# Opening PSUM sums by ScalarE copies and splitting B in place, in a hybrid state-space and attention kernel

## The chip, the cores and the metric

The kernel runs on one core of a Trainium2 chip. The metric is the device time of one execution in microseconds (us). The five engines are called by their short names: PE (TensorE, matmuls; its weight loads are PEld), DVE (VectorE), ACT (ScalarE), POOL (GpSimd) and SP (SyncE, which issues all the DMAs). SBUF is the working memory; PSUM is the small memory of 8 banks that matmuls write and add into.

## The reference

The network has four layers over an image batch of shape (4, 64, 64, 96). Layers 0 and 1 are selective state-space blocks, layers 2 and 3 are linear attention with a quantised feed-forward block. Nearly all of the time is in layers 0 and 1. Layer 0, cut to what matters (layer 1 differs in its four orders of the pixels):

```python
xz = x @ in_proj_w.T
xi, z = jnp.split(xz, 2, axis=-1)
xc = silu(conv3x3_depthwise(xi) + conv_b)             # 192 channels, 4096 pixels
xs = four orders of xc                                # rows, columns, and both reversed
dts, Bs, Cs = jnp.split(einsum('bkdl,kcd->bkcl', xs, x_proj_w), [R, R + N], axis=2)
delta = softplus(einsum('bkrl,kdr->bkdl', dts, dt_w) + dt_b)

def step(h, inp):                                     # N = 16 states per channel
    u_t, dt_t, B_t, C_t = inp
    h = exp(dt_t[..., None] * A) * h + (dt_t * u_t)[..., None] * B_t[:, :, None, :]
    return h, einsum('bkdn,bkn->bkd', h, C_t)

out_y = ys + Ds * xs
y = sum of the four orders of out_y, each put back in image order
y = layer_norm(y) * silu(z) @ out_proj_w.T
```

The sum over the four orders k of `Ds * xs` is, in image order, `(sum of Ds over k) * xc`. The sum y of a pixel thus starts from that product and takes in 4 orders of 16 states each.

## The kernel before, in words

**Tiling.** Two images share the 128 partitions, 64 channels each, and the 192 channels make J = 3 chunks j. A phase is one of the two layers with one pair of images, so there are 4 phases. In a phase the loops run over k (4 orders) and t (4 stretches of TB = 1024 pixels); one (phase, k, t) is a block, 64 in all. A block has 48 tiles: two groups g of 8 states, for each the chunks j, and in each of those 8 tiles n. A tile of 128 x 1024 holds two states of one image. That makes 3072 tiles, and a **boundary** after every 8 tiles, 384 sums in all.

**One tile i** passes through these instructions, each on a fixed engine:

- the decay `exp(delta * a)`, ACT, line 692 (`decays`), into the tile f or, for 5 of 16 states (`POOL_N` = 1, 4, 7, 10, 13), into PSUM psB;
- the input `du * B`. For the 11 other states PE spreads the row of B over the partitions into psB (line 685, `row`, a bf16 matmul with selector weights), and DVE multiplies by du (line 699, `product`). For the 5 of `POOL_N`, POOL multiplies with rows that a DMA spread (line 675, `begin`);
- the scan along the 1024 pixels, DVE, line 707, and a copy of its last column for the next block, ACT, line 713;
- the weighting by C, POOL, line 718 (`weigh`), in place in f. There are 6 buffers of f;
- after every second tile, the gather: PE adds the two states of both tiles into the sum tile psY (line 750, 4 fp32 matmuls, 8 instructions in the records).

**The sum tile.** psY takes two PSUM banks, and there is one of it. The other six banks are two psB of two banks each and two psM of one bank each. After 8 tiles `flush` copies psY out on ACT: after the first group into an SBUF tile ysum (line 762); after the second back into image order into ynew (line 766, in one to four pieces by the order) and on to DRAM. Then `resume` reopens psY for the next group with what was summed before, by matmuls with `start=True` (line 741, PE): ysum with the identity for g = 1; for g = 0, the old sum yold, which a DMA brought in (`recall`, line 727), in the order of this k, again with the identity; and for the first k the conv's output, with the diagonal matrix dg of summed Ds.

**Order of the work.** PE, DVE, ACT and POOL execute their instructions in the order in which the program writes them; only SP's order is left to the scheduler. The main loop, at step i, writes: the decay of tile i+2 (`begin`), the flush of i-3 if it ends a group, the gather of i-2 (for odd n), the row of i+2, the scan of i, the POOL_N decay of i+2, the product of i+1, the weighting of i, then the preparation of the next block (`prepare`, a table of places in the block), a piece of the aside work, and last of all `resume` of i-2 if that begins a group. The aside work is the convolution of a later phase and the layer norm, gate and output projection of the one before; it needs psM tiles, and takes none during the places at which `prepare` needs them.

**The split of B.** `prepare` projects xs to B, C and dt rows in a psM tile (line 565), copies them out (`rows`, line 576), and cuts B into three bf16 parts whose sum is B (`cut`, line 582, ACT). Between the cuts `take` makes the remainder: a fresh psM tile, B in fp32 by the identity (line 587), minus the parts so far (line 588). The `steps` (line 592) with `biased` (599) and softplus (605) give delta, `inputs` (608, POOL) gives delta times x.

After the last tile come the attention and feed-forward layers, written by a small planner at build time that uses the same PSUM tiles.

Of the kernel before, what the change touches and what calls it, by code (L numbers as in the profile page):

```python
# [8 lines left out]
F32 = mybir.dt.float32  # L9
# [8 lines left out]
N = 16  # L18
# [16 lines left out]
def kernel(ctx: ExitStack, tc: tile.TileContext, ins, out, layers=(0, 1, 2, 3)):  # L35
# [8 lines left out]
    def st(shape, dtype, tag, bufs, name=None):  # L44
        return sp.tile(shape, dtype, tag=tag, name=name or tag, bufs=bufs)
# [7 lines left out]
    def psM(shape):  # L53
        return ps.tile(shape, F32, tag="psM", name="psM", bufs=2)
# [18 lines left out]
    def small(shape, name, dtype=F32):  # L73
        return st(shape, dtype, name, 2, name)
# [74 lines left out]

    def skips(li):  # L150

        dsum = small([128, J, 1], "dsum")
        nc.vector.reduce_sum(dsum, W[li]["ds"], axis=mybir.AxisListType.X)
        dg = W[li]["dg"] = st([128, J, 128], F32, "dg", 1)
        for j in range(J):
            nc.scalar.activation(dg[:, j, :], ident, AF.Copy, scale=dsum[:, j, :])

    def tail_weights(li):

# [312 lines left out]
    def pieces(li, k, t):  # L472

        if li == 0:
            if k in (0, 2):
                tt = t if k == 0 else NTB - 1 - t
                img = lambda v: v[:, tt * TB : (tt + 1) * TB]
                view = lambda v: v if k == 0 else v[:, ::-1]  # L480
                return img, [(view, lambda o: o)], lambda py, v: [
                    (py[:, s * T : (s + 1) * T], view(v)[:, s * T : (s + 1) * T]) for s in range(2)
                ]
            cols = TB // HW
            tt = t if k == 1 else NTB - 1 - t
            img = lambda v: v.rearrange("p (h w) -> p h w", w=HW)[:, :, tt * cols : (tt + 1) * cols]

            def view(v):
                v = v.rearrange("p h w -> p w h")
                return v if k == 1 else v[:, ::-1, ::-1]  # L490

            return img, [(view, lambda o: o.rearrange("p (w h) -> p w h", h=HW))], lambda py, v: [
                (py[:, s * T : (s + 1) * T], view(v)[:, s * cols // 2 : (s + 1) * cols // 2]) for s in range(2)
            ]
        img = lambda v: v[:, t * TB : (t + 1) * TB]
        if k == 0:
            return img, [(lambda v: v, lambda o: o)], None
        s = 1 << k
        n = TB // (s * HW)

        def by_row(r):
            return (
                lambda v: v.rearrange("p (a i b j) -> p i a b j", i=s, j=s, b=HW // s)[:, r],
                lambda o: o.rearrange("p (a b i j) -> p i a b j", i=s, j=s, b=HW // s)[:, r],
            )

        def by_band(a):
            return (
                lambda v: v.rearrange("p (a i b j) -> p a b i j", i=s, j=s, b=HW // s)[:, a],
                lambda o: o.rearrange("p (a b i j) -> p a b i j", i=s, j=s, b=HW // s)[:, a],  # L510
            )

        def resumed(py, v):
            v = v.rearrange("p (a i b j) -> p a b i j", i=s, j=s, b=HW // s)
            return [(py[:, a * TB // n : (a + 1) * TB // n], v[:, a]) for a in range(n)]

        return img, [by_row(r) for r in range(s)] if s < n else [by_band(a) for a in range(n)], resumed

    def imaged(li, k, v):

# [2 lines left out]
    def prepare(ph, k, t):  # L523
# [2 lines left out]


        li = phases[ph][0]
        img, views, resumed = pieces(li, k, t)
        p = {"views": views, "img": img, "resumed": resumed, "dus": [None] * J, "deltas": [None] * J}  # L530
        xs, deltas = [], []
        halves = [slice(s * T, (s + 1) * T) for s in range(2)]
        raws, pps, rests, pds = [], [], [], []
        taken = {}

        def weights():
            if li not in W:
                W[li] = scan_weights(li)
            if t == 0 and k == 0 and "dg" not in W[li]:
                skips(li)  # L540
            if t == 0:
                xp = st([128, J, 76], F32, "xp", 1)
                nc.sync.dma_start(xp, ins[f"L{li}_xp"][k])
                dtw = st([76, J, 128], F32, "dtw", 1)
                nc.sync.dma_start(dtw[64:76], ins[f"L{li}_dtw"][k])
                order[0] = (xp, dtw)
# [31 lines left out]
            nc.sync.dma_start(p["bc"][:, halves[s]], rests[s][0 : 4 * N])  # L578

        def cut(s, q):  # L580
            of = taken.pop(s) if q else pps[s][0 : 2 * N]
            nc.scalar.copy(p["parts"][32 * q : 32 * q + 32, halves[s]], of)

        def take(s, q):
            of = taken[s] = psM([2 * N, T])
            part = slice(0, 32 * q + 32)
            nc.tensor.matmul(of, ident[0 : 2 * N, 0 : 2 * N], rests[s][0 : 2 * N], start=True, stop=False)
            nc.tensor.matmul(of, minus[part], p["parts"][part, halves[s]], start=False, stop=True)

        def steps(s, j):  # L590
            pds.append(psM([128, T]))
# [128 lines left out]

    def recall(i):
        at, g, j, n = tiles[i]
        ph, k, t = blocks[at]
        sums[at, j] = imaged(phases[ph][0], k, part([128, TB], "yold"))
        nc.sync.dma_start(sums[at, j], made[at]["img"]((yd if k else xcd)[ph][:, j, :]))

    def resume(i):
        at, g, j, n = tiles[i]  # L730
        ph, k, t = blocks[at]
        py = sums[at, g, j] = psY()
        old = sums.pop((at, j))
        of = W[phases[ph][0]]["dg"][:, j, :] if g == 0 and k == 0 else ident
        if g == 0 and k:
            parts = made[at]["resumed"](py, old)
        else:
            parts = [(py[:, s * T : (s + 1) * T], old[:, s * T : (s + 1) * T]) for s in range(2)]
        banks = len(parts) * T // TB
        for m, (o, v) in enumerate(parts):  # L740
            nc.tensor.matmul(o, of, v, start=(m % banks == 0), stop=False)  # L741

    def gather(i):
        at, g, j, n = tiles[i]
        py = sums[at, g, j]
        two = [scanned.pop(e)[1] for e in (i - 1, i)]
        for s in range(2):
            ss = slice(s * T, (s + 1) * T)
            for e in range(2):
                nc.tensor.matmul(  # L750
                    py[64 * e : 64 * e + 64, ss], fold, two[e][:, ss],
                    start=False, stop=(n == g * GN + GN - 1),
                )

    def flush(i):
# [283 lines left out]
    end = len(tiles)  # L1039
    now, rest = [0], (L - TB) // 256  # L1040
    with tc.manual_schedule(engines=MANUAL):
        convs = [conv(0)]
        while done[0][0] < TB // T:
            next(convs[0])
# [24 lines left out]
        for i in range(-9, end + 4):  # L1069
# [5 lines left out]
                begin(i + 2)  # L1075
            if 0 <= i - 3 < end and tiles[i - 3][3] % GN == GN - 1:
                flush(i - 3)
            if 0 <= i - 2 < end and tiles[i - 2][3] % 2:
                gather(i - 2)
            if 0 <= i + 2 < end:  # L1080
# [11 lines left out]
            if 0 <= i < end:  # L1092
# [21 lines left out]
                if aside is not None and not (plan and place in kept) and (holds[0] or holds[1] <= room):  # L1114
                    advance()
                    if holds[2] and (late_by(i, blocks[at][0]) or holds[0] >= room):
                        advance()
            if 0 <= i - 2 < end and tiles[i - 2][3] % GN == 0:
                resume(i - 2)
        now[0] = end + per  # L1120

        def remaining():
# [113 lines left out]
```

## Time and profile before

| what | value |
|---|---|
| median of 3 runs | 11,311.74 us (11,305.0 to 11,312.93) |
| the profiled execution | 11,302.74 us |
| its span, from the first instruction to the last | 11,301.0 us |
| scan stage, first to last weighting | 139 to 10,674 us |
| POOL busy | 10,203.7 us |
| DVE busy | 9,943.6 us |
| PE busy | 9,004.1 us |
| ACT busy | 6,635.3 us |
| granted TensorE clock, mean | 0.856 |

The page gives, per engine, the time in which it executed something; an engine that waits for another is idle. A row of the groups names the line, the engine, the operation and the tiles written and read, then the count, the busy time and the mean of one in ns, and behind the bar the idle time of the engine ahead of those instructions with what ended most of it. The matmul times include the pipeline, so neighbours overlap a little. An fp32 matmul shows as two instructions.

### The profile page before, as it was taken

The page shows a single profiled execution, that of the slowest core. Times are in us where ns is not written, and L with a number is a line of the kernel's source. Part 1 is how long each engine was busy: PE and PEld are TensorE (multiplying, and loading weights), DVE is VectorE, ACT ScalarE, POOL GpSimd, SP SyncE. Part 2 cuts the span into 40 slices and gives each one's busy share as a digit, 9 for nine tenths or more (in the row PEclk, how much of TensorE's full clock was granted, in tenths as well). Part 3 has the DMA queues.
Part 4 walks back from the last instruction along what each step waited for, and adds up shares of the span by engine and source line. Part 5 has one row for each costly group of instructions (what it writes and reads, how often), then busy time and mean ns, then how long its engine had stood idle before and what let it go on. Part 6 is the DMA issues. An engine that isn't in the chain of part 4 may idle for free. (4 is left out here: it accounts for less than half of the span.)

```text
span 11301.0 us, 102140 instructions
## 1 busy us (share of the span) xinstructions
PE 9004.1 (80%) x30112; PEld 2910.9 (26%) x30112; DVE 9943.6 (88%) x6431; ACT 6635.3 (59%) x10733; POOL 10203.7 (90%) x5102
## 2 busy tenths in 40 slices
PE   7878888777777877888777777888778887777776
PEld 2212222111222222222222222222222232222365
DVE  4888999999999899988999999999989899999835
ACT  3656666554556655666555655666555555555676
POOL 3889999999999999989999998999999999999846
PEclk8989898888888888988888888999888888888877
DMA  5669876897678886799656556665566565556410
GB/s 131 154 137 158 141 154 155 152 135 135 151 162 143 140 159 155 152 142 148 149 146 159 156 138 150 159 167 146 143 157 156 140 157 146 138 139 154 123 39 18
DMA packets 1848989, 1605.36 MB, mean 142 GB/s; under 512 B 1412330, under 2 KB 1483692, under 8 KB 1848428
## 3 DMA queue, kind: packets, MB, share of 16 engines
q1 hardware_dynamic: 1848428, 1598.83, 65.1%
q8 instruction: 237, 3.88, 0.2%
q14 instruction: 324, 2.65, 0.1%
HBM read 1009.16 MB, written 186.65 MB: 106 GB/s over the span
## 5 line engine op out<-in xcount | busy, mean ns | idle before, releaser
L718 POOL TENSOR_TENSOR f<-f,crep 128x1024 f32<-128x1024 f32 x3072 | 7165.4, 2356 | 522.9 <-DVE f L707 413.0
L707 DVE TENSOR_TENSOR_SCAN f<-f,state,psB 128x1024 f32<-128x1024 f32 x1584 | 3718.0, 2347 | 210.4 <-ACT f L692 48.0
L750 PE MATMUL psY<-f,fold 128*64 128x512 f32 x12288 | 3771.4, 701 | 161.0 <-POOL f L718 160.3
L692 ACT ACTIVATE f<-delta,L_a 128x1024 f32<-128x1024 f32 x2112 | 2408.6, 1145 | 988.1 <-PE psY L750 897.8
L699 DVE TENSOR_TENSOR psB<-psB,du 128x1024 f32<-128x1024 f32 x2112 | 2558.5, 1211 | 458.9 <-PE psB L685 405.1
L685 PE MATMUL psB<-spB,sel 96*128 96x512 bf16 x4224 | 1406.9, 420 | 1626.0 <-DVE f L707 1595.8
L675 POOL TENSOR_TENSOR f<-du,brep 128x1024 f32<-128x1024 f32 x960 | 2266.9, 2361 | 169.5 <-DMA crep<-bc 39.2
L707 DVE TENSOR_TENSOR_SCAN f<-psB,state,f 128x1024 f32<-128x1024 f32 x720 | 1677.0, 2329 | 123.7 <-ACT psB L692 86.6
L713 ACT COPY state<-f 128x1 f32<-128x1 f32 x2304 | 430.4, 187 | 2048.2 <-DVE f L707 2037.5
L750 PEld LDWEIGHTS psY<-f,fold 128*64 128x64 f32 x12288 | 952.7, 155 | 2524.2 <-issue 1818.0
L692 ACT ACTIVATE psB<-delta,L_a 128x1024 f32<-128x1024 f32 x960 | 1070.7, 1115 | 625.0 <-DVE f L707 576.8
L707 DVE TENSOR_TENSOR_SCAN f<-f,psB 128x1024 f32<-128x1024 f32 x528 | 1207.6, 2287 | 55.1 <-ACT f L692 5.1
L685 PEld LDWEIGHTS <-sel 96*128 96x128 bf16 x4224 | 274.5, 99 | 3320.8 <-DVE f L707 2106.4
L300 PE MATMUL psM<-pad,wf 96*64 96x512 f32 x3456 | 872.7, 622 | 7.1 <-ACT pad L290 4.0
L741 PE MATMUL psY<-ysum,ident 128*128 128x512 f32 x768 | 589.5, 912 | 73.3 <-ACT ynew L766 60.2
L707 DVE TENSOR_TENSOR_SCAN f<-psB,f 128x1024 f32<-128x1024 f32 x240 | 545.7, 2274 | 78.4 <-ACT psB L692 46.5
L608 POOL TENSOR_TENSOR xs<-delta,xs 128x1024 f32<-128x1024 f32 x192 | 453.0, 2359 | 93.6 <-ACT delta L605 93.6
L741 PE MATMUL psY<-yold,ident 128*128 128x512 f32 (+2 forms) x960 | 388.5, 547 | 129.9 <-ACT ysum L762 98.3
L592 PE MATMUL psM<-proj,dtw 12*128 12x512 f32 x768 | 456.5, 688 | 0.0
L565 PE MATMUL psM<-xs,xp 128*76 128x512 f32 x768 | 417.7, 655 | 10.1 <-DMA xp<-in_L_xp 4.1
L766 ACT COPY ynew<-psY 128x1024 f32<-128x1024 f32 (+2 forms) x312 | 242.3, 818 | 188.7 <-PE psY L750 188.7
L300 PEld LDWEIGHTS psM<-pad,wf 96*64 96x64 f32 x3456 | 223.5, 139 | 475.9 <-issue 448.0
(150 smaller groups left out, 6946.9 us busy)
## 6 DMA issues: line engine op xcount, KB each, us to landing
crep<-bc SPq DMA_DIRECT2D x2048, 256.0 KB
delta<-delta SPq DMA_DIRECT2D x768, 256.0 KB
du<-xs SPq DMA_DIRECT2D x768, 256.0 KB
brep<-bc SPq DMA_DIRECT2D x640, 256.0 KB
yd<-ynew SPq DMA_DIRECT2D x192, 512.0 KB
xraw<-xcd SPq DMA_DIRECT2D x144, 512.0 KB
yold<-yd SPq DMA_DIRECT2D x144, 512.0 KB
yu<-yd SPq DMA_DIRECT2D x65, 384.0 KB
```

The costliest lines, as they stand in the source:

```text
L300: nc.tensor.matmul(px[64 * i : 64 * i + 64], w["wf"][:, tap, 64 * j : 64 * j + 64], pads[i][0][:, tap // 3 : tap // 3 + rows, tap % 3 : ta ...
L592: nc.tensor.matmul(pds[-1], order[0][1][64:76, j, :], rests[s][64:76], start=True, stop=True)
L608: nc.gpsimd.tensor_mul(xs[j], deltas[j], xs[j])
L675: nc.gpsimd.tensor_mul(f[:, 1:], made[at]["dus"][j][n % 2], reps[at, 0, n])
L685: nc.tensor.matmul(scanned[i][0][:, ss], sel[:, n, :], made[at]["parts"][:, ss], start=True, stop=True)
L692: nc.scalar.activation(out, made[at]["deltas"][j][n % 2], AF.Exp, scale=W[phases[ph][0]]["a"][:, k, j, n // 2 : n // 2 + 1])
L699: nc.vector.tensor_mul(scanned[i][0], scanned[i][0], made[at]["dus"][j][n % 2])
L707: nc.vector.tensor_tensor_scan(f[:, 1:], a, bu, 0.0 if t == 0 else states[at - 1][:, c : c + 1], ALU.mult, ALU.add)
L713: nc.scalar.copy(states[at][:, c : c + 1], f[:, TB : TB + 1])
L718: nc.gpsimd.tensor_mul(f[:, 0:TB], f[:, 1:], reps[at, 1, n])
L741: nc.tensor.matmul(o, of, v, start=(m % banks == 0), stop=False)
L750: nc.tensor.matmul(py[64 * e : 64 * e + 64, ss], fold, two[e][:, ss], start=False, stop=(n == g * GN + GN - 1),)
```

## The change

- `resume` no longer uses PE. ACT writes the old sum into psY: a plain copy of ysum for g = 1; a copy with the scale dsum, one number per partition, for g = 0 of the first k; and for g = 0 of the other k one to four copies that read yold in this k's order. The gathers then add to what ACT wrote, with `start=False`.
- `resume` is written right after the flush in the step, ahead of the gather, and no longer at its end.
- `unlock` runs once at the start: 8 matmuls of the identity over psY, so that the later matmuls with `start=False` add to what is in the banks.
- The matrices dg (3 activations for each of the two layers) are no longer made; the sums dsum are kept.
- `take` no longer uses a second psM tile nor the identity matmul. It subtracts the one part cut last from the projection itself, in its PSUM tile, and the next cut reads it there.
- In the instruction streams DVE and POOL have the same instructions in the same order; PE loses 960 matmuls of resumes and 256 of takes and gains the 8; ACT gains 504 copies. SP issues the same 5,798 DMAs with some in other places.

```diff
     def skips(li):
-        dsum = small([128, J, 1], "dsum")
+        dsum = W[li]["skip"] = small([128, J, 1], "dsum")
         nc.vector.reduce_sum(dsum, W[li]["ds"], axis=mybir.AxisListType.X)
-        dg = W[li]["dg"] = st([128, J, 128], F32, "dg", 1)
-        for j in range(J):
-            nc.scalar.activation(dg[:, j, :], ident, AF.Copy, scale=dsum[:, j, :])
...
         def cut(s, q):
-            of = taken.pop(s) if q else pps[s][0 : 2 * N]
-            nc.scalar.copy(p["parts"][32 * q : 32 * q + 32, halves[s]], of)
+            nc.scalar.copy(p["parts"][32 * q : 32 * q + 32, halves[s]], pps[s][0 : 2 * N])
 
         def take(s, q):
-            of = taken[s] = psM([2 * N, T])
-            part = slice(0, 32 * q + 32)
-            nc.tensor.matmul(of, ident[0 : 2 * N, 0 : 2 * N], rests[s][0 : 2 * N], start=True, stop=False)
-            nc.tensor.matmul(of, minus[part], p["parts"][part, halves[s]], start=False, stop=True)
+            part = slice(32 * q, 32 * q + 32)
+            nc.tensor.matmul(
+                pps[s][0 : 2 * N], minus[part], p["parts"][part, halves[s]], start=False, stop=True,
+                skip_group_check=True,
+            )
...
+    def unlock():
+        py = psY()
+        for s in range(2):
+            for q in range(T // 128):
+                o = s * T + q * 128
+                nc.tensor.matmul(py[:, o : o + 128], ident, ident, start=(q == 0), stop=True, skip_group_check=True)
...
     def resume(i):
         py = sums[at, g, j] = psY()
         old = sums.pop((at, j))
-        of = W[phases[ph][0]]["dg"][:, j, :] if g == 0 and k == 0 else ident
-        if g == 0 and k:
-            parts = made[at]["resumed"](py, old)
+        if g:
+            nc.scalar.copy(py, old)
+        elif k == 0:
+            nc.scalar.activation(py, old, AF.Copy, scale=W[phases[ph][0]]["skip"][:, j, :])
         else:
-            parts = [(py[:, s * T : (s + 1) * T], old[:, s * T : (s + 1) * T]) for s in range(2)]
-        banks = len(parts) * T // TB
-        for m, (o, v) in enumerate(parts):
-            nc.tensor.matmul(o, of, v, start=(m % banks == 0), stop=False)
+            for src, dst in made[at]["views"]:
+                nc.scalar.copy(dst(py), src(old))
...
+        unlock()
         convs = [conv(0)]
...
                 flush(i - 3)
+            if 0 <= i - 3 < end and tiles[i - 3][3] % GN == GN - 1 and i - 2 < end or i == 2:
+                resume(i - 2)
             if 0 <= i - 2 < end and tiles[i - 2][3] % 2:
                 gather(i - 2)
...
-            if 0 <= i - 2 < end and tiles[i - 2][3] % GN == 0:
-                resume(i - 2)
```

## The prediction

> **What bounds the kernel now.** I read the busy times first, then the same over the scan stage alone (from the first weighting at 139 us to the last at 10,674 us, with the tail and attention after it), then the groups, the waits, and one stretch of the timeline.
>
> ```profile
> PE 9004.1 (80%) x30112; PEld 2910.9 (26%) x30112; DVE 9943.6 (88%) x6431; ACT 6635.3 (59%) x10733; POOL 10203.7 (90%) x5102
> ```
> ```profile
> 139.00:10674.00 10535.00, 8461.81 (x26558) 2505.68 (x26557) 9626.13 (x5543) 6170.27 (x9610) 9843.73 (x4338) 0.86 0.69 149
> ```
>
> The columns of the second are length, then PE, PEld, DVE, ACT, POOL busy, then the granted clock. In the stage POOL is idle 10,535 − 9,844 = 691 us and DVE 909 us. Neither the order nor the work of these two changes, so **691 us is the most that a better feed can give** unless work on them gets shorter. PE at 80% is no bound by its sum; it matters by being late.
>
> ```profile
> L718 POOL TENSOR_TENSOR f<-f,crep 128x1024 f32<-128x1024 f32 x3072 | 7165.4, 2356 | 522.9 <-DVE f L707 413.0
> ...
> L750 PE MATMUL psY<-f,fold 128*64 128x512 f32 x12288 | 3771.4, 701 | 161.0 <-POOL f L718 160.3
> ...
> L699 DVE TENSOR_TENSOR psB<-psB,du 128x1024 f32<-128x1024 f32 x2112 | 2558.5, 1211 | 458.9 <-PE psB L685 405.1
> ...
> L741 PE MATMUL psY<-ysum,ident 128*128 128x512 f32 x768 | 589.5, 912 | 73.3 <-ACT ynew L766 60.2
> ```
>
> The last field is idle time ahead of the group and who ended it. POOL waits for DVE's scan (413 us); DVE waits for PE's row broadcast L685 (405 us). Why is PE late? At a group boundary (every 8 tiles, 384 in all) PE reopens the sum by identity matmuls (L741) after ScalarE has emptied the one psY tile (L762, L766), and in PE's order the next gather L750 and the row L685 stand behind that. One such place on the timeline, PE first, then DVE, then POOL:
>
> ```profile
> 5758.77 3.78 PE L741 MATMUL psY<-ysum,ident 128*128 128x512 f32 x4 [2.46 <-ACT ynew L766]
> 5762.48 3.11 PE L750 MATMUL psY<-f,fold 128*64 128x512 f32 x8
> 5765.52 0.61 PE L685 MATMUL psB<-spB,sel 96*128 96x512 bf16 x2
> ```
> ```profile
> 5761.30 2.35 DVE L707 TENSOR_TENSOR_SCAN f<-psB,state,f 128x1024 f32<-128x1024 f32 x1 [1.10 <-ACT psB L692]
> 5766.17 1.23 DVE L699 TENSOR_TENSOR psB<-psB,du 128x1024 f32<-128x1024 f32 x1 [2.52 <-PE psB L685]
> ```
> ```profile
> 5770.74 2.35 POOL L718 TENSOR_TENSOR f<-f,crep 128x1024 f32<-128x1024 f32 x1 [2.15 <-DVE f L707]
> ```
>
> Columns: start, length, engine, line; in brackets the idle time before and its releaser. The flush L766 had run from 5757.72 to 5758.71. The reopening takes 3.78 us, the gather ends 8 us after the flush began, the product waits 2.52 us for the row behind it, and POOL 2.15 us soon after.
>
> **The change, part by part.**
>
> *The opening moves from PE to ACT.* In the trace's records I paired each of 383 boundaries' flush, reopening and gather. The reopening starts 1.09 us after the flush ended (mean) and lasts 2.82 us. The gather begins with its end every time, on average 4.3 us after the weightings it needs were finished: the reopening is the last input at 382 of 383. Now a ScalarE copy follows the flush at once; the gather waits for that copy instead, and queued behind the gather on PE is, as before, the row L685, for which DVE's product waits. ScalarE into PSUM is seen as L692 psB (1.115 us, Exp), the reverse copy as L762 (1.006 us); permuted flushes L766 as 1.36 us mean (120), 0.58 (512 columns), 0.38 (256 columns). Taken: 240 plain at 1.006; 72 of layer 0 permuted at 1.6 (from L766: (120×1.359 − 48×1.006)/72); layer 1: 96 pieces at 0.58, 96 at 0.379. Sum 241 + 115 + 56 + 36 = **448 us more on ACT** (59% to 63%). With 1.0 or 1.6 us per boundary the gather can begin 2.43 us earlier on average.
>
> Not all of it stays. From the instructions of tile psY:
>
> ```profile
> L750 PE MATMUL psY<-f,fold x12288: 590/592/1117, 145.9 to 10675.4; 128*64 128x512 f32 x199
> ...
> L741 PE MATMUL psY<-ysum,ident x768: 590/1057/1223, 269.8 to 10657.9; 128*128 128x512 f32 x192
> ```
>
> Shortest, median and longest in ns: the ysum reopening mostly runs at half clock, the gather behind it at full. Half of all reopenings (50%) took over 2.9 us. Without them the gather is the first work after PE's wait and takes 3.6 us for 2.08: 0.5×1.5 = 0.7 us lost, 1.72 us left per boundary.
>
> What is felt: I followed every idle gap of POOL in the stage back over its releasers for 16 us. 218 gaps, 271 us, pass through L741, at 135 boundaries. Cutting each boundary at what its gather's end can gain leaves 200 us. Another input is late next (the aside work on PE, ACT's exponentials), so I take 85%: **−170 us**. Ends: 0 (all hidden behind those) and −271.
>
> The trace's clock record shows 487 drops to half in the stage, 2,854 us (27%), in multiples of 3.41 us; PE was busy 42% of the 3.41 us before a drop, 81% at random places. The Trainium skill, "TensorE: Matmul & The Clock Gate", Part 1, says that the clock halves after an idle window of about 3.4 us. The window's length agrees; that it must be idle does not, a thinly used one is enough here. By the page's rule removing reopenings would cost no clock and the term would be 85% of 247, −210; by the rows it is the −170 above, and that speaks against the change.
>
> *ACT's queue.* Behind the new copy wait the state copy L713, the decays L692, cuts L582 and the aside work's copies. I pushed each boundary's following ACT instructions by the copy until idle time took it up, and compared each exponential's end with its scan's start: 83 scans are pushed, 65 us together (in the place above, the 1.10 us wait at 5761.30 becomes about 2.1). Part falls where POOL has work in hand: **+40**, ends 0 and +65. The copy itself waits for nothing new: psY is freed by the same engine, and the loads of yold were issued 12.7 us or more (median 35) before the flush's end, with no wait on them shown.
>
> *take: one matmul for two.* 256 times the fp32 identity matmul L587 goes (512 instructions, 272 us busy, 0.53 us each), and L588 adds onto the projection; it waits for the cut before it, as it did. The chain cut–take–cut stands between a projection and the steps; DVE gaps whose chain (10 us back) holds L588 sum to 69 us, POOL's to 11. Taken: **−25**, ends 0 and −69. The projection's psM tile is held longer, until the third cut, but nothing of the aside work runs in those places.
>
> *At nothing:* the dg tile's 6 activations; unlock's 16 matmul instructions (at L367's 287 ns 4.6 us) lie before 17.03 us, PE's first work, and would cost those 4.6 us if PE were needed then. SP's order: 2,031 of 5,798 issues change place, 99% by 10 or fewer. POOL's waits ended by a DMA sum to 83 us, DVE's to 46; I take 0, ends ±40.
>
> Sum: −170 + 40 − 25 = −155. The profiled execution took 11,302.74 us (span 11,301.0), so 11,148; the median of the runs is 9 us higher, and every case below stands against that median of 11,311.7. **Forecast 11,157 us.**
>
> **The rivals.**
> - *Cold gathers.* With 1,357 us less work (1,085 + 272) PE falls to half clock more often and every gather runs cold: 1.5 us lost at each boundary. The capped sum is then 185 us; with rows late too, half is felt: −93 + 40 − 25 = −78, **11,234**. For it: the 42%; against: in conv blocks PE stays full.
> - *PE's backlog goes.* The aside convolutions and tails queue on PE, and 1,357 us less lets half of the 691 idle go: −346, **10,966**. For it: counted by block, POOL idles some 2 us in blocks without aside work (the ninth to thirteenth, say) and about 10 in those with it. Against: most gaps do not pass through L741.
> - *ACT takes PE's place, slower.* Right behind the flush, where softplus or conv copies keep ACT full, the exponential of a POOL tile comes late by the whole copy, and the scan with it. From 195 us of pushed scans (170 + 25, 43% of the copies) the gain is gone; the trace has 65. At 70%, 314 − 195 = +119: **11,431**. For it: exponential n=4 has under 0.21 us of slack before its scan in a tenth of the tiles; against: its median is 1.9 us.
> - *No change.* The instruction streams do what the diff says, but the product may wait anyway, for the previous scan or the weighting: the −170 shrinks to −20, the −25 to nothing, and of the +40 some 20 remain: 0, **11,312**.
>
> **How the numbers follow.** Forecast 0.44, cold gathers 0.20, backlog 0.13, ACT 0.15, no change 0.08. About 0.2% (23 us) can be told from no change: faster 0.76, same 0.09, slower 0.15. The range goes from 10,970 (all of the 271 and the 69 and no loss: −340) to 11,340 (the same −170, with ACT's pushes at three times 65: +195, so +25); it leaves out most of ACT's case and about half of the backlog's.
>
> **What would show it.** Right: no matmul between flush and gather; gathers beginning 1 to 2 us after the flush's end; L699's wait for L685 falling from 405 us to some 250; POOL's stage idle from 691 to about 540; L750's mean rising above 701 ns. Wrong: L707's wait for ACT L692 growing from 188 us by over 150; or POOL's idle staying at 690 with another releaser.

## The result and the profile after

The changed kernel takes 11,298.22 us in the median (11,281.56 to 11,319.88, 20 runs), the kernel before, on the same chip, 11,302.02 us (11,290.81 to 11,313.71, 20 runs). The ratio is 0.9998, 95% interval 0.9991 to 1.0005: **no change** that can be measured, where 11,157 us was forecast. The profiled execution took 11,291.57 us (span 11,289.8).

First the busy times, then the scan stage alone (columns as before: length, PE, PEld, DVE, ACT, POOL busy, granted clock):

```profile
PE 8418.7 (75%) x27696; PEld 2658.3 (24%) x27696; DVE 9945.0 (88%) x6431; ACT 7094.3 (63%) x11231; POOL 10199.5 (90%) x5102
```
```profile
136.00:10668.00 10532.00, 7883.93 (x24136) 2256.42 (x24137) 9626.61 (x5544) 6630.09 (x10111) 9837.11 (x4338) 0.82 0.68 149
```

ACT's busy time grew by 459 us (448 were worked out). PE's fell by only 585 us, though the matmuls that the change takes out had been counted at 1,357 us: what stayed ran longer, the gathers alone by 490 us (4,261.9 for 3,771.4). POOL's idle time in the stage is 10,532 − 9,837 = 695 us, where it was 691. The groups of the weighting, the gather, the product and the steps:

```profile
L705 POOL TENSOR_TENSOR f<-f,crep 128x1024 f32<-128x1024 f32 x3072 | 7159.4, 2354 | 482.4 <-DVE f L694 354.0 <-issue 39.8 <-DMA crep<-bc 18.7
L745 PE MATMUL psY<-f,fold 128*64 128x512 f32 x12288 | 4261.9, 771 | 675.3 <-issue 292.9 <-POOL f L705 281.5 <-POOL f L662 91.8
...
L686 DVE TENSOR_TENSOR psB<-psB,du 128x1024 f32<-128x1024 f32 x2112 | 2558.2, 1211 | 368.2 <-PE psB L672 327.2 <-DMA du<-xs 31.8 <-DMA crep<-bc 5.0
...
L579 PE MATMUL psM<-proj,dtw 12*128 12x512 f32 x768 | 526.4, 783 | 0.2 <-ACT spB L568 0.2
```

POOL waits less for the scan (413 to 354 us), DVE's product less for the row (405 to 327). The gather grew from 701 to 771 ns a piece, and the steps from 688 to 783. What the two waits gave up stands in four other rows of the waits (columns: who waits, for whom, us, times, longest):

```profile
DVE f L694 <- ACT psB L679: 191.7, 70, 29.4
...
POOL f L662 <- DMA crep<-bc: 81.0, 54, 4.3
...
DVE f L694 <- ACT f L679: 72.0, 50, 8.0
...
POOL f L662 <- DMA du<-xs: 54.4, 15, 7.0
```

The same four in the kernel before:

```profile
DVE f L707 <- ACT psB L692: 134.9, 47, 27.7
...
DVE f L707 <- ACT f L692: 53.1, 34, 6.3
...
POOL f L675 <- DMA crep<-bc: 39.2, 22, 3.9
...
POOL f L675 <- DMA du<-xs: 33.9, 10, 4.4
```

The first two are the scan's waits for the exponentials into psB and into f, the others `begin`'s waits for DMAs. ACT's share thus grew by 76 us, that of these DMAs by 62. The same boundary as in the prediction shows it in small (PE, then ACT, DVE, POOL, from the timeline after):

```profile
5763.94 3.64 PE L745 MATMUL psY<-f,fold 128*64 128x512 f32 x8 [3.55 <-POOL f L662]
5767.51 0.61 PE L672 MATMUL psB<-spB,sel 96*128 96x512 bf16 x2
```
```profile
5761.80 0.99 ACT L761 COPY ynew<-psY 128x1024 f32<-128x1024 f32 x1
5762.82 1.02 ACT L731 COPY psY<-ysum 128x1024 f32<-128x1024 f32 x1
...
5765.23 1.12 ACT L679 ACTIVATE psB<-delta,L_a 128x1024 f32<-128x1024 f32 x1
```
```profile
5766.45 2.35 DVE L694 TENSOR_TENSOR_SCAN f<-psB,state,f 128x1024 f32<-128x1024 f32 x1 [2.17 <-ACT psB L679]
5768.71 1.21 DVE L686 TENSOR_TENSOR psB<-psB,du 128x1024 f32<-128x1024 f32 x1
```
```profile
5768.88 2.36 POOL L705 TENSOR_TENSOR f<-f,crep 128x1024 f32<-128x1024 f32 x1 [0.86 <-DVE f L694]
```

The gather begins 1.15 us after the flush and not 3.77; the product no longer waits for the row (2.52 us before). But the exponential stands behind the opening copy, and the scan waits 2.17 us for it, where it waited 1.10. POOL's gap is 0.86 us for 2.15. So this place gained; over the 383 boundaries the gather ends 4.51 us after the flush, where it was 5.92. The question is where the gain went.

### The profile page after: what moved, and what is told of

Same layout as the page of the kernel before. It is cut to its first block, busy times and chain, and to the rows that moved or that the text cites. A ratio compares the mean times of both kernels' runs of the same rounds, so it can differ in the third digit from the quotient of the medians.

```text
span 11289.8 us, 97780 instructions
## 1 busy us (share of the span) xinstructions
PE 8418.7 (75%) x27696; PEld 2658.3 (24%) x27696; DVE 9945.0 (88%) x6431; ACT 7094.3 (63%) x11231; POOL 10199.5 (90%) x5102
## 5 line engine op out<-in xcount | busy, mean ns | idle before, releaser
L745 PE MATMUL psY<-f,fold 128*64 128x512 f32 x12288 | 4261.9, 771 | 675.3 <-issue 292.9
L672 PE MATMUL psB<-spB,sel 96*128 96x512 bf16 x4224 | 1484.2, 439 | 1927.9 <-DVE f L694 1878.9
L745 PEld LDWEIGHTS psY<-f,fold 128*64 128x64 f32 x12288 | 1079.3, 166 | 3138.4 <-issue 2189.0
L297 PE MATMUL psM<-pad,wf 96*64 96x512 f32 x3456 | 912.9, 645 | 11.6 <-ACT pad L287 8.4
L579 PE MATMUL psM<-proj,dtw 12*128 12x512 f32 x768 | 526.4, 783 | 0.2 <-ACT spB L568 0.2
L586 ACT ACTIVATE delta<-psM,L_dtb 128x512 f32<-128x512 f32 x384 | 261.3, 681 | 144.3 <-PE psM L579 143.7
```

The lines of the kernel that those rows point to most:

```text
L297: nc.tensor.matmul(px[64 * i : 64 * i + 64], w["wf"][:, tap, 64 * j : 64 * j + 64], pads[i][0][:, tap // 3 : tap // 3 + rows, tap % 3 : ta ...
L579: nc.tensor.matmul(pds[-1], order[0][1][64:76, j, :], rests[s][64:76], start=True, stop=True)
L672: nc.tensor.matmul(scanned[i][0][:, ss], sel[:, n, :], made[at]["parts"][:, ss], start=True, stop=True)
L745: nc.tensor.matmul(py[64 * e : 64 * e + 64, ss], fold, two[e][:, ss], start=False, stop=(n == g * GN + GN - 1), skip_group_check=True,)
```

## The experiments

The theories. **Level:** PE's reopening is one of several inputs that are late by nearly the same; taking it away uncovers the next, so the gain was small from the start. **ACT:** the gain is there, and ACT's longer queue takes it. **Split:** the gain is there, and the split in place takes it through PE's pauses. **SP:** the DMAs that changed place take it. All kernels are compared with the kernel before, run on the same chip, where its median was 11,302 to 11,310 us in the five sets of runs. So runs of different sets are compared by their ratios, and a difference in us is the ratio times 11,302 unless the text says medians. "Idle" is POOL's idle time in the stage of the profiled execution (from the records, first weighting to last), "end" the mean time from a flush's end to the end of the next gather (left out where the flush goes by halves).

| kernel | median us | ratio, 95% interval | idle us | end us | clock |
|---|---|---|---|---|---|
| before | 11,302.02 | 1 | 691 | 5.92 | 0.856 |
| after | 11,298.22 | 0.9998 (0.9991 to 1.0005) | 695 | 4.51 | 0.814 |
| open_alone | 11,280.15 | 0.9978 (0.9969 to 0.9987) | 660 | 4.42 | 0.823 |
| take_alone | 11,355.09 | 1.0046 (1.0034 to 1.0059) | 739 | 5.73 | 0.851 |
| no_open | 11,254.34 | 0.9960 (0.9948 to 0.9973) | 655 | 3.79 | 0.811 |
| open_twice | 11,484.43 | 1.0166 (1.0152 to 1.0180) | 881 | 5.83 | 0.800 |
| take_warm | 11,322.34 | 1.0016 (1.0007 to 1.0025) | 710 | 5.70 | 0.858 |
| open_halves | 11,318.41 | 1.0016 (1.0007 to 1.0024) | 710 | | 0.808 |
| sp_before | 11,528.10 | 1.0193 (1.0176 to 1.0210) | 855 | 5.92 | 0.848 |
| sp_open | 11,487.84 | 1.0164 (1.0149 to 1.0180) | 803 | 4.47 | 0.815 |
| gross | 11,257.71 | 0.9957 (0.9944 to 0.9969) | 648 | 3.82 | 0.809 |
| gross_act | 11,301.22 | 0.9996 (0.9987 to 1.0005) | 693 | 3.82 | 0.815 |
| late2 | 11,281.58 | 0.9978 (0.9969 to 0.9986) | 660 | 3.82 | 0.862 |
| late1 | 11,266.75 | 0.9963 (0.9949 to 0.9976) | 660 | 4.06 | 0.863 |
| after_warm | 11,319.41 | 1.0015 (1.0006 to 1.0024) | 718 | 4.42 | 0.817 |
| pe_twice | 11,696.40 | 1.0348 (1.0334 to 1.0362) | 1086 | 7.74 | 0.871 |

### The two halves of the change

**open_alone**: the change with the old `take` and `cut`.

> Of the change only the opening by ScalarE's copies, with the old split of B (two matmuls and a second psM tile). Theory 1, the opening gains at the boundaries but ACT's copies and a colder PE take it back: 11,290 to 11,330 us, first gathers about 2.8 us long, DVE's waits for ACT's exponentials near 260 us as in the changed kernel (188 before). Theory 2, the opening was hidden anyway because POOL and DVE bind each other: within 20 us of before, with all the waits only moved. Theory 3, SP's changed order of DMAs costs what the opening gains: here SP's order differs from both kernels in other places, so POOL's waits ended by a DMA (83 us before, 135 in the changed kernel) move and the time with them by about as much.

Measured: 0.9978, 25 us faster, a little more than the first two theories had it (11,290 to 11,330 us, and within 20 us of before). The scan's waits for ACT are 269 us, as theory 1 had it.

**take_alone**: the kernel before with the new `take` and `cut` only.

```diff
-            part = slice(0, 32 * q + 32)
-            nc.tensor.matmul(of, ident[0 : 2 * N, 0 : 2 * N], rests[s][0 : 2 * N], start=True, stop=False)
-            nc.tensor.matmul(of, minus[part], p["parts"][part, halves[s]], start=False, stop=True)
+            part = slice(32 * q, 32 * q + 32)
+            nc.tensor.matmul(pps[s][0 : 2 * N], minus[part], p["parts"][part, halves[s]], start=False, stop=True, ...)
```

> Of the change only the split of B in place on the projection; the sums are opened by PE as before. Theory 1: a small gain, 5 to 30 us (11,270 to 11,295), the 272 us of PE work leaving. Theory 2: within 10 us of before. Theory 3: the time follows POOL's waits ended by a DMA, up by tens of us if they rise as in the changed kernel, though nothing at the boundaries changed.

Measured: 1.0046, 52 us slower, though PE has 256 matmuls less; none of the three theories had that. POOL's waits that a DMA ended, over all its instructions in the stage, are 92 us in both kernels, so nothing speaks for theory 3. In the groups the steps' mean rose from 688 to 753 ns and ACT's wait for them from 39.2 to 122.2 us:

```profile
L592 PE MATMUL psM<-proj,dtw 12*128 12x512 f32 x768 | 504.4, 753 | 0.0
...
L599 ACT ACTIVATE delta<-psM,L_dtb 128x512 f32<-128x512 f32 x384 | 261.5, 681 | 122.6 <-PE psM L592 122.2
```

On the timeline of take_alone, behind a split:

```profile
6399.04 0.98 PE L685 MATMUL psB<-spB,sel 96*128 96x512 bf16 x2 [3.90 <-DVE f L707]
...
6399.96 2.07 PE L592 MATMUL psM<-proj,dtw 12*128 12x512 f32 x2
...
6406.39 1.23 DVE L699 TENSOR_TENSOR psB<-psB,du 128x1024 f32<-128x1024 f32 x1 [1.59 <-PE psB L685]
```

PE idles for 3.90 us, the two step matmuls then take 2.07 us, and a row late behind them makes the product wait 1.59 us. In the kernel before the identity matmul (L587) stands in the corresponding pause, and the same steps take 1.12 us:

```profile
6372.85 1.04 PE L587 MATMUL psM<-proj,ident 32*32 32x512 f32 x2
...
6373.82 0.39 PE L588 MATMUL psM<-spB,minus 64*32 64x512 bf16 x1
...
6374.14 0.60 PE L685 MATMUL psB<-spB,sel 96*128 96x512 bf16 x2
...
6374.67 1.12 PE L592 MATMUL psM<-proj,dtw 12*128 12x512 f32 x2
```

### Is it the opening's price?

**no_open**: the changed kernel without any opening (the gathers start the sum themselves, and the old sums are missing).

```diff
-        if g:
-            nc.scalar.copy(py, old)
...
-                    start=False, stop=(n == g * GN + GN - 1), skip_group_check=True,
+                    start=(n == g * GN + 1), stop=(n == g * GN + GN - 1), skip_group_check=True,
```

> The changed kernel without any opening: the copies of ScalarE are left out and the first gather of a group starts the sum (the old sums are not added, so only the last group's part remains). This is the opening at a price of nothing on any engine. Theory 1: ACT's 448 us go, so 100 to 170 us faster than the changed kernel (11,130 to 11,200). Theory 2: within 30 us of 11,300; then no way of opening is worth anything. Theory 3: some gain, but POOL's waits ended by a DMA stay at 130 us or more.

Measured: 0.9960, some 45 us under the kernel before. This is 43 us under the changed kernel, short of theory 1's 100 us and more than theory 2's 30.

**open_twice**: the changed kernel with every opening copy written twice (for the first k a plain copy ahead of the scaled one).

```diff
             nc.scalar.copy(py, old)
+            nc.scalar.copy(py, old)
```

> The changed kernel with every opening copy made twice, so 448 us more on ACT and each opening 1.2 us longer. Theory 1: ACT's copies are dear, 60 to 200 us slower than the changed kernel (11,360 to 11,500). Theory 2: within 30 us of the changed kernel. Theory 3: SP's order is that of the run with the opening alone, and the time differs from that run's by ACT's cost only.

Measured: 442 us more ACT cost some 190 us against the changed kernel (1.0166 against 0.9998); the scan's wait for psB's exponential rose from 191.7 to 349.4 us:

```profile
DVE f L694 <- ACT psB L679: 349.4, 162, 30.7
```

The second opening costs far more than the first does. But the gather also ends 1.31 us later (5.83 us for 4.51), so this run does not tell ACT's queue from the later gather; gross_act, below, does.

**open_halves**: open_alone with psY as two tiles of one bank; flush and opening by halves, the first gather pieces follow the first half.

```diff
+    ybank = [ps.tile([128, T], F32, tag=f"psY{h}", name="psY", bufs=1) for h in range(2)]
...
-            nc.scalar.copy(sums[at, j], py)
+            for h in range(2):
+                nc.scalar.copy(ys[:, h * T : h * T + T], py[h])
+                yield
```

> The run with the opening alone (11,280 us), with the sum in two tiles of one bank: ScalarE flushes and opens the first bank, then the second, so the gather's first half may start about 1.1 us earlier, and PE idles less at the boundary. ScalarE pays some 0.15 us for each extra instruction, about 110 us in all. Theory 1 (the wait of PE and its cold clock eat the opening's gain, ScalarE's load the rest): 20 to 60 us faster than the run with the opening alone, first gathers nearer to full clock. Theory 2 (hidden behind DVE and POOL): no more than 15 us from it either way. If ScalarE's load decides, 20 to 50 us slower.

Measured: 1.0016, 43 us slower than open_alone. More and shorter copies on ACT cost more than a gather that may begin after the first half brings.

**gross**: open_alone with the opening left out: nobody opens, the old sums are missing, and the old `take` stays. **gross_act**: the same, but ACT copies the old sum onto itself, a weight that nothing waits for.

```diff
-        if g:
-            nc.scalar.copy(py, old)
...
+        nc.scalar.copy(old, old)      (gross_act only)
```

> The run with the opening alone and the old split of B, but with the opening left out: no copies, the first gather of a group starts the sum (the old sums are not added, so only the last group's part remains). It is what the boundary can give at most, at no price on any engine and without the other part of the change. By the two runs before (50 us for the opening left out, 50 us the price of the split in place) it is 11,200 to 11,230 us, 80 to 100 us below before. If the prediction's 170 us were there before the prices: 11,140. If nothing is there: 11,290 or more.

> The same with ScalarE's load put back as dead weight: each old sum is copied onto itself at the place of the opening, one plain copy of 128 x 1024, and no engine waits for it (the sums stay incomplete as in the run before). If ScalarE's queue is the price of the opening, this stands 40 to 70 us above the run without the copies and within 20 us of the run with the opening alone (11,280). If PE's wait for the copy, and the cold clock after it, are the price, it stays within 15 us of the run without copies.

Measured: gross is 49 us under the kernel before (0.9957). That is the opening's **whole** worth in this kernel when PE loses it and no engine takes it, with gathers ending 2.10 us earlier at each boundary; PE's clock falls with it, to 0.809. From the two runs before 80 to 100 us had been expected: the price of the split in place does not come back here, since with it and without an opening (no_open) the time is the same. gross_act is 44 us slower than gross (medians) for 337 us of copies, with gathers that end as early: ACT's queue has a price of its own. At the boundary shown above gross has no gap left on POOL: it runs three instructions in a row.

```profile
5742.82 3.68 PE L739 MATMUL psY<-f,fold 128*64 128x512 f32 x8 [2.55 <-ACT state L701]
...
5743.25 6.99 POOL L706 TENSOR_TENSOR f<-f,crep 128x1024 f32<-128x1024 f32 x3
```

So the local gain is complete here. I counted POOL's idle time by the tile's place in the block. At the six places where boundaries show (6, 14, 22, 30, 38 and 46 of 48) it fell from 252 us before to 135 in gross, −117; at the other 42 it grew from 439 to 513, +74. Two thirds of the gain are given back. The largest single return is place 24, where the second group begins (26 to 58 us); the waits that grew are the scan's for the two exponentials (188 to 232 us) and `begin`'s for the DMAs of crep, du and brep (83 to 104 us). From the waits of gross:

```profile
DVE f L695 <- ACT psB L680: 142.1, 50, 29.4
ACT delta L587 <- PE psM L580: 137.4, 121, 3.6
...
DVE f L695 <- ACT f L680: 89.8, 42, 7.6
```

Two things speak against reading these 74 us as the next inputs alone. Place 24 rises as much in take_alone (to 59) and in pe_twice below (to 54), which are both slower than before. And PE is colder in gross: ACT waits 137.4 us for the step matmuls, 39.2 before. No run leaves the opening out and keeps PE's clock, so what part of the returns the colder PE makes is not shown.

### From the other side

**pe_twice**: the kernel before with each reopening made twice on PE.

```diff
-        for m, (o, v) in enumerate(parts):
-            nc.tensor.matmul(o, of, v, start=(m % banks == 0), stop=False)
+        for m, (o, v) in enumerate(parts + parts):
+            nc.tensor.matmul(o, of, v, start=(m % banks == 0), stop=(m < len(parts) and m % banks == banks - 1))
```

> The kernel before with every reopening made twice on PE (the second with start=True again): PE gets 1,085 us more, and each gather begins some 2.8 us later. It asks how steep the time is in the opening's own time. Leaving the opening out gave 49 us. Theory level (the opening is one of several inputs that are late by nearly the same, so that taking it away uncovers the next): a second opening has nothing beside it that is as late, and costs several times 49: +150 to +400 us, POOL's idle time growing by as much, 11,450 to 11,700. Theory slack (the opening is mostly beside the path, and what it costs is a fixed share of its time): about as much again as the first, +30 to +70 us. The prediction's reading (85% of the attributed gaps) would have been +170 or more on both sides, and the first half of that has already failed.

Measured: 1.0348, 393 us slower, with PE busy 626 us longer (9,630.1 for 9,004.1). Two groups of pe_twice:

```profile
L718 POOL TENSOR_TENSOR f<-f,crep 128x1024 f32<-128x1024 f32 x3072 | 7169.9, 2357 | 832.7 <-DVE f L707 663.6 <-issue 111.3 <-POOL f L718 18.2
...
L699 DVE TENSOR_TENSOR psB<-psB,du 128x1024 f32<-128x1024 f32 x2112 | 2562.1, 1213 | 909.9 <-PE psB L685 858.5 <-DMA du<-xs 38.6 <-DMA crep<-bc 5.9
```

The product's wait for the row doubles, 405 to 858 us, and POOL's idle time grows by 395 us, the whole loss. Set the two sides beside each other. Gathers that end 2.10 us earlier at 383 boundaries (804 us) bring 49 us, 6%. Gathers that end 1.82 us later (697 us) cost 393 us, 56%. The time has a **kink** at the place where the kernel before stands. This is what the theory of the level says; a fixed felt share (the prediction's 85%, or a small one) does not have it. The colder PE may flatten the side of the gain; against it, late2 below has gathers that end as early as gross's at a clock of 0.862 and gains 25 us, though its identity matmuls still stand in PE's queue.

### The same gain without ACT

**late2** and **late1**: the kernel before, in which the first gather starts the sum (`start=True`), and the identity matmuls add the old sum later, behind the first gather and the row: late2 in two pieces, late1 in one. The sum is the same but for its order, PE's work is the same, ACT's does not grow.

```diff
+            for o, of, v in late_adds.pop(i, ()):
+                nc.tensor.matmul(o, of, v, start=False, stop=False, skip_group_check=True)
...
-                    start=False, stop=(n == g * GN + GN - 1),
+                    start=(n == g * GN + 1), stop=(n == g * GN + GN - 1), skip_group_check=True,
```

> The kernel before with the opening on PE, as it was, but later: the first gather of a group starts the sum, and the identity matmuls add the old sum two and four tiles after, one bank each time, where nobody waits for them. Nothing is on ScalarE, PE keeps its work and with it its clock. If the boundary's wait was the cost and PE's clock and ScalarE's load took the change's gain back, this is the best of all: 60 to 110 us below before (11,195 to 11,245), clock near 0.85, DVE's wait for PE's rows falling from 405 us to 300 or less. If PE's whole time is what counts, or the boundary is hidden anyway: within 25 us of before.

> The same with all identity matmuls of a boundary in one place, behind the first gather and the row that follows it, one tile after. The work comes in a piece of 2 to 3.7 us while rows are still due, so 0 to 40 us slower than the run with two pieces, but still below before.

Measured: 0.9978 and 0.9963. late2 had been expected 60 to 110 us under before, and late1 behind late2; neither came. **late1, 42 us (27 to 58) under the kernel before, is the fastest of the versions that compute all**, and beats both kernels. It has nearly all of gross's 49. Its timeline at our boundary:

```profile
5744.34 3.26 PE L751 MATMUL psY<-f,fold 128*64 128x512 f32 x8 [2.55 <-ACT state L714]
5747.53 1.98 PE L1123 MATMUL psY<-ysum,ident 128*128 128x512 f32 x4
5749.35 0.60 PE L686 MATMUL psB<-spB,sel 96*128 96x512 bf16 x2
```

The gather follows the flush, and the identity matmuls run behind it in 1.98 us (3.78 before); no row stands between, as POOL makes the next input here. The idle time of late1 fell at other places than gross's, though: the six boundary places keep 241 us of 252, place 24 falls from 26 to 6. Which of the several small waits it relieves was not separated.

### SP's order, and PE's pauses

**sp_before**, **sp_open**: the kernel before and open_alone with SP's DMAs in the order in which the program writes them, so that both issue alike (the two traces have one order throughout).

```diff
-MANUAL = {mybir.EngineType.PE, mybir.EngineType.DVE, mybir.EngineType.Activation, mybir.EngineType.Pool}
+MANUAL = {mybir.EngineType.PE, ..., mybir.EngineType.Pool, mybir.EngineType.SP}
```

> The kernel before, with SP's DMAs too in the order in which the program writes them, as the other engines. It fixes one order for this pair of runs. Theory 3: the pair with the opening alone in the same order then shows the opening's gain without SP's reordering. By itself, no theory says more than that a DMA waiting at the head of the queue holds back the rows behind it: between 50 us faster and 300 us slower than before.

> The run with the opening alone with SP's DMAs in program order, to be held against the run of the kernel before in that order: the two issue the same DMAs in the same order. Theory 3, SP's order took back the gain: 60 to 150 us faster than that one, and POOL's waits ended by a DMA equal. Theory 1: 10 to 50 us faster, as without the fixed order (25 us). Theory 2: within 15 us.

Measured: both are some 2% slower, so the scheduler's order is worth about 200 us. Under equal orders the opening brings 40 us (medians 11,528.10 to 11,487.84), with free ones 25. The difference of 15 us is inside the intervals (each about ±0.0016, or 18 us): SP's order is not what took the gain, and a small part can't be excluded.

**take_warm**: take_alone plus an identity matmul of the removed one's shape into an unused quarter of the same PSUM tile. **after_warm**: the changed kernel with the same.

```diff
-                pps.append(psM([76, T]))
+                pps.append(psM([128, T]))
...
+            nc.tensor.matmul(
+                pps[s][96:128], ident[0 : 2 * N, 0 : 2 * N], rests[s][0 : 2 * N], start=True, stop=True, ...
```

> The run with the split of B in place alone (11,355 us, 50 us slower than before) with one dead matmul added behind each subtraction: the identity matmul that the change took away, of the same shape and cost, written into the fourth quarter of the same PSUM bank, where nobody reads it. 272 us of useless PE work comes back, nothing else. Theory 1, the split in place is slower because PE idles there, falls to half clock and runs the following steps and gathers cold: the time falls back by 30 to 60 us to 11,295 to 11,325, ScalarE's wait for the steps from 122 us towards 40, and steps from 753 ns towards 690. Theory 2, the split in place itself is slower (the projection's tile is held longer, or its ScalarE reads and PE writes of one bank disturb each other): 11,350 or more, as the dead work can only add. Theory 3, SP's order: the time follows POOL's waits ended by a DMA (97 us in the run with the split alone), whatever PE does.

> The changed kernel, with a useless fp32 identity matmul beside each in-place subtraction, into an unused quarter of the same PSUM tile: PE gets back the 272 us of work that the split in place took away, nothing waits for its result. Theory clock (the split in place costs because PE pauses at the split, its clock halves, and the steps and gathers after it run cold): it gains here as it did with the old opening, about 33 us, to some 11,265 us; L579-type step matmuls return from 783 ns towards 740 and DVE's wait for the row from 327 us towards 290. Theory ACT (with the opening on ACT the split's cost is hidden behind ACT's waits, since the whole change is only 18 us above the opening alone): within 10 us of the changed kernel, 11,290 to 11,310.

Measured: the useless matmul makes take_alone 34 us **faster** (1.0046 to 1.0016); the steps return to 712 ns, ACT's wait for them to 96.2 us (towards 40 had been expected):

```profile
ACT delta L603 <- PE psM L596: 96.2, 93, 2.0
```

The DMA orders of the two traces differ in 9 of 5,796 places, so SP's order is not the reason. So with the old opening some two thirds of the split's price (34 of 52 us, give or take 17) come from PE doing nothing where it had work; the rest is open. In the changed kernel the same matmul makes it 19 us **slower** (0.9998 to 1.0015), the steps gain little (783 to 765 ns) and the clock hardly moves (0.814 to 0.817). There the theory of the pauses does not hold, and the theory of ACT, which had the time within 10 us, does not either.

## Why the prediction was wrong

**The step that failed** is "What is felt": "Cutting each boundary at what its gather's end can gain leaves 200 us. Another input is late next ..., so I take 85%: −170 us." The gross gain, measured without any price, is 49 us, a quarter of the 200. Following a gap back to the reopening tells that PE released it last; it does not tell how much earlier the second-latest input was. The prediction named the next inputs, and priced them at 15%, with no row for it. The runs show in its place that without the reopening only 117 us went at the boundary's own places, and that 74 came back at others, behind exponentials and DMA rows. The kink (49 us on one side, 393 on the other) points the same way without any attribution. That the returns follow because POOL and DVE, freed at one place, run up against the next input sooner is argued from this; each return was not tested alone, and the colder PE can have a part in them.

**Point by point.**

- *The boundary itself* was right. Gathers begin 1.70 us after the flush's end (3.84 before), last 2.81 us (2.08 before; the predicted 0.7 us for a cold one), and end 1.41 us earlier; 1.72 had been taken.
- *The 85% of 200 us:* −49 instead of −170, inside the ends 0 to −271, which the range held.
- *ACT's queue, +40* (0 to +65): right within its ends. 337 us of dead copies cost 44; in place the opening's copies leave 25 of gross's 49, so cost 24 (each give or take some 18). ACT's added 459 us were taken as 448.
- *take, −25:* wrong in sign. Alone it costs 52 us; on top of ACT's opening 23 (0.9978 to 0.9998, give or take 13 for the two intervals); without any opening nothing that can be told (gross 0.9957, no_open 0.9960). The prediction priced the shorter chain and not PE's pause, which by take_warm makes some two thirds of the first case. It did name PE's thinly used stretches, but weighed them only for the gathers.
- *SP's order, 0 ± 40:* held, as far as it can be told.
- *The sum,* in measured terms: −49 + 24 + 23 = −2 us, against −170 + 40 − 25. The three are the steps from before by gross and open_alone to the changed kernel, so they have to add up; what they show is where the 170 went.
- *The rivals.* "No change" was the outcome, at 0.08. Its main mechanism, that the product and POOL wait anyway for another input, fits the small gross gain (−49, where it had −20); but its zero also took the split in place as free, and in the runs the split's price of 23 us is what closes the sum. "Cold gathers" was right about the clock (gathers of 2.81 us, and below). The cold clock's cost was not measured apart: late1 and gross differ by 0.863 and 0.809 in the clock and by 9 us in time, but late1 still has the identity matmuls. "PE's backlog goes" is out: no_open leaves out all 1,357 us of PE's work that the rival counted on, and gains 45. "ACT takes PE's place" is out in size: the scan's waits for ACT grew by 76 us, not by 150.
- *What would show it.* Right were the gather's start and its mean of 771 ns. Of the reopening no matmul is left between flush and gather, but other work of PE starts there at 229 of the 383 boundaries. The wait for the row fell to 327 and not to 250. What had been named as a sign of error came: POOL's idle time stayed at 690 with other releasers.

**Open:** why the split in place costs 23 us with ACT's opening, where PE's pauses are not the reason, how much of gross's returns the colder PE makes, and which of late1's relieved waits counts.

## What to carry to other kernels

Idle time that a trace lays at one instruction's door is what that instruction released last, and an upper bound: before a price is paid for its removal, measure what leaving it out altogether brings (the gross gain, here 49 us of 200), and what making it longer costs (393 us), since a kernel whose inputs arrive nearly level can lose steeply on one side and gain little on the other, as this one does. Where a late input is only a start value of a sum, adding it later on the same engine can bring the gain without loading another one (late1, 0.9963).

## What the runs showed of the hardware

- PE's clock follows how its work is spread as well as its sum. From before to after the drops to half clock between the first and the last weighting rose from 492 to 605 and their time from 2,884 to 3,799 us (the prediction's 487 and 2,854 are a little short). The clock changes only at the ends of windows of 3.41 us. In the kernel before there are 275 windows at full clock in which PE was busy less than 40%, and after every one of them the clock halved; no window that kept it was under 41%. Each of the 492 returns to full clock followed a window at least 70% busy. The busy share alone does not decide, since 149 drops followed windows that were half busy or more.
- So the windows ahead of a drop need not be idle. The Trainium skill, "TensorE: Matmul & The Clock Gate", Part 1, speaks of an idle window there; in the sixteen traces these windows were 31 to 42% busy on average (42% before, 33% after).
- More PE work can raise the clock: in pe_twice it is 0.871, and the reopenings by ysum, mostly at half clock before (median 1,057 ns), run at 593, though half of them are the second of a pair:

```profile
L741 PE MATMUL psY<-ysum,ident x1536: 590/593/1222, 276.6 to 11070.0; 128*128 128x512 f32 x192
```

- Dead PE work can pay: a matmul that nobody reads took 34 us off take_alone. It is no rule, since it added 19 us to the changed kernel.
- ScalarE writes PSUM about as fast as it reads it: a median of 1,017 ns for the 128x1024 copy from ysum into psY, 1,012 for the copy out. Matmuls with `start=False` add to what it wrote, after the opening matmuls at the start.
- The order of SP's issues alone is worth about 2%: the same DMAs (5,796 issues in each trace) in program order cost 11,528.10 us against 11,307.57.
